# The seam between output projection and second MLP: first weights unpacked inside the join's loop, the last tiles turned at other places, other banks and another order of products

## The chip, the cores and the metric

The kernel runs on one core of a Trainium2 chip. The metric is the device time of one execution in microseconds (us). Engines are named as in the profile: PE is TensorE's matrix multiply and PEld its weight load, DVE is VectorE, ACT is ScalarE, POOL is GpSimd, and SP is SyncE, which issues nearly all DMAs here. L215 means line 215 of the kernel.

## The reference, cut to what matters

Two residual layers on x of shape 2 x 1024 x 512 (2048 tokens, 16 tiles of 128 tokens), all in float32:

```
xn = layernorm(x)
s  = delta_rule_attention(xn)            # 16 heads of 128, then o @ Wo
g  = silu(ternary_mlp(xn))               # inner width 1408
x  = x + s * g
xn = layernorm(x)
s  = rg_lru(xn)                          # block-diagonal gates, softplus(a_param), a scan over time
g  = silu(nvfp4_mlp(xn))                 # inner width 4096, 4-bit codes with a scale per block of 32
x  = x + s * g
```

The seam of this case is the line in the middle: the output projection `o @ Wo`, its product with g, the sum with x and the layernorm, and the beginning of the second layer's MLP.

## The kernel before

**First layer.** A long loop over units of the attention computes the heads' outputs and writes them to a DRAM buffer `od`; the first MLP runs woven into it and leaves its gated result in `gd`. This loop is planned by the kernel's own code and isn't touched by the diff.

**The join** (class `Join`). For each of the 16 tiles of tokens (two batches alternate, `self.order`), `product` (L186 on) multiplies the 16 heads' outputs by the resident `wo`, in 16 matmuls of 128x128 by 128x512 (two records each) that add up in one PSUM bank `jpo`. Then `rest` holds the steps after it: `jg = jg * jpo` (L215, DVE), `jx = jg + jx` (L211, DVE; a DMA writes it to `x1d`), statistics of the layernorm (L206 to L208, DVE), `ln_rs = ve ** -0.5` (L218, POOL), and the norm, written over `jg` (L219, DVE). `turn` transposes the normed tile twice on PE (`ptr`, L113, 4 + 4 matmuls): one copy (ACT, L117) goes to DRAM `xd` for the recurrence, one (DVE, L119) goes into the "quarters" `xq[b]` that the second MLP reads, and for every second tile of a batch four DVE adds (L261 to L264) make sums of these quarters. The first three tiles' products are made at the end of the attention's loop, woven into it; `Join.run` (L222) does the rest, a tile per iteration, with loads of `jo` (L173), `jx` (L182) and `jg` (L184) two or three tiles ahead. In an iteration `run` issues product i, the steps of `rest`, and then, as `late`, the turn of tile i-1, so on PE the transposes of tile i-1 stand behind the whole product i. The norm of the last tile is a tile of its own, `xn_last`, and its turn is returned and done by the second layer.

**Second layer** (`second_layer`, L1079). The MLP's 4096 inner columns are worked off in 16 groups. A group's weights w_g, w_u and w_d come as 4-bit codes `pk` with scales `sc`; `unpack` (L1119) loads both and then yields after each of seven DVE operations (five on the codes' bits, with `hi` as a second buffer, and two multiplications by `sc`), after which POOL makes four sums of blocks of the weights (3.65 us in all). The products are of a Strassen kind: seven products of quarters, so that weights and `xq` each exist in seven pieces. A half step n of the main loop (L1441 on; 32 of them, group n // 2, batch n % 2) is the gate's seven products and the up projection's seven, 14 slots in all. In each slot the code takes one product, one piece of the down projection of the half step before (`downs`), one step of the next group's unpacking (`steps`), and pieces of the recurrence, which has 16 chunks that start at half steps set by `starts` (`recur`). From `order["on"] = True` on, engines do their instructions in the order in which the program writes them (class `Ordered`, whose helper line L130 is the line of all of these in the profile); ahead of that a scheduler of the compiler's framework places them. In the last group the sums of the down projection's seven parts, `together`, are put between, one per slot.

Ahead of the main loop stand, in this order: the first group's unpacking (three weights, 24 steps), loads of `bd` and `vec`, and `softplus` (L87 on) of `vec`: two ACT functions and some 18 small DVE operations on 128x4. PSUM pools are `l1_psh` (banks of the gate and up products: pga, pgb, pgc, pua, pub, puc), `l1_pso` and `l1_psr`, allocated in this order; they take the place of the join's banks.

The names that the change touches are `Join.run`, `Join.turn`, `second_layer` with `unpack`, `quartered`, `halved` and `group_weights`, and its main loop.

Of the kernel before, what the change touches and what calls it, by code (L numbers as in the profile page):

```python
# [4 lines left out]

# [7 lines left out]
F32 = mybir.dt.float32  # L13
# [4 lines left out]
ALU = mybir.AluOpType  # L18
PSUM = bass.MemoryType.PSUM
DRAM = bass.MemoryType.DRAM  # L20

P = 128
B, T, D = 2, 1024, 512
NT = B * T
KC = D // P
NTT = NT // P
H = 16
# [35 lines left out]
def done(steps):  # L63
    for _ in steps:
        pass
# [72 lines left out]
class Join:  # L138
# [86 lines left out]
    def run(self, xd, xq, xp):  # L225

        nc, tc = self.tc.nc, self.tc
        with self.ctx as ctx:
            ps_o, ps_t = (
                ctx.enter_context(tc.tile_pool(name=n, bufs=bufs, space=PSUM, reuse_waits="tile"))  # L230
                for n, bufs in (("j_pso", 3), ("j_pst", 2))
            )
            late = None
            for i in range(NTT):
                if i >= self.made:
                    for _ in range(min(i + 3, NTT) - len(self.o)):
                        self.load_o()
                    done(self.product(ps_o, "pso", nc.tensor.matmul))
                    g = self.xg[i][1]
                    if i == NTT - 1:  # L240
                        g = xp.tile([P, D], F32, name="xn_last")
                    for step in self.rest(g):
                        step()
                if late is not None:
                    late(ps_t, "pst", self.xg[i - 1][0].rearrange("p (k t) -> p k t", k=KC))
                    for _ in range(min(i + 3, NTT) - len(self.xg)):
                        self.load_xg()
                g = g if i == NTT - 1 else self.xg[i][1]
                late = functools.partial(self.turn, xd, xq, *self.order[i], g)
        return late  # L250

    def turn(self, xd, xq, c, b, g, psp, tag, xt):
        nc, ident = self.tc.nc, self.cst[:, C_ID, :]
        transposed(nc, psp, tag, xt, g, ident, "scalar")
        nc.sync.dma_start(xd[b].rearrange("k p t -> p k t")[:, :, c * P : (c + 1) * P], xt)
        h, cols = c % 2, slice(c // 2 * P, (c // 2 + 1) * P)
        quarters = xq[b][:, 0:4].rearrange("p (kc h) par t -> p h kc par t", h=2)[:, h, :, :, cols]
        transposed(nc, psp, tag, quarters, g, ident, "vector", step=2)
        if h:
            b11, b12, b21, b22, t1, t2, t4 = (xq[b][:, q, :, cols] for q in range(7))  # L260
            nc.vector.tensor_tensor(t1, b12, b11, ALU.subtract)  # L261
            nc.vector.tensor_tensor(t2, b22, t1, ALU.subtract)
            nc.vector.tensor_tensor(t4, b21, t2, ALU.subtract)
            nc.vector.tensor_tensor(b12, b22, b12, ALU.subtract)  # L264
# [814 lines left out]
def second_layer(ctx, tc, a, cst, x1d, xd, xq, out, late):  # L1079
# [18 lines left out]
    nc = tc.nc  # L1098
    cp = ctx.enter_context(tc.tile_pool(name="l1_c", bufs=1, reuse_waits="tile"))
    rp = ctx.enter_context(tc.tile_pool(name="l1_r", bufs=1, reuse_waits="tile"))  # L1100
    wp = ctx.enter_context(tc.tile_pool(name="l1_w", bufs=2, side="right", reuse_waits="tile"))
    qp = ctx.enter_context(tc.tile_pool(name="l1_q", bufs=2, side="right", reuse_waits="tile"))
    hp = ctx.enter_context(tc.tile_pool(name="l1_h", bufs=1, reuse_waits="tile"))
    ps_h = ctx.enter_context(tc.tile_pool(name="l1_psh", bufs=1, space=PSUM, reuse_waits="tile"))
    ps_o = ctx.enter_context(tc.tile_pool(name="l1_pso", bufs=2, space=PSUM, reuse_waits="tile"))
    ps_r = ctx.enter_context(tc.tile_pool(name="l1_psr", bufs=2, space=PSUM, reuse_waits="tile"))
    yd = tc.dram_tile([NT, D], F32, name="yd")
    ident = cst[:, C_ID, :]
    order = {"on": False}
    PE, DVE, ACT, POOL = (  # L1110
        Ordered(tc, e, lambda: order["on"]) for e in (nc.tensor, nc.vector, nc.scalar, nc.gpsimd)
    )
    A11, A12, S3, A22, S1, S2, S4 = range(7)
    B11, T3, B21, B22, T1, T2, T4 = range(7)

    def unpack(name, g, dst, sums):  # L1119

        pk = qp.tile([P, 512], I32, tag="pk", name=f"pk_{name}_{g}")
        nc.sync.dma_start(pk, a[name + "pk"][g])
        sc = qp.tile([P, 512], F32, tag="sc", name=f"sc_{name}_{g}")
        nc.sync.dma_start(sc, a[name + "sc"][g])
        yield
        hi = qp.tile([P, 512], I32, tag="hi", name=f"hi_{name}_{g}", bufs=1)
        DVE.tensor_scalar(hi, pk, 0xF0, 12, ALU.bitwise_and, ALU.logical_shift_left)
        yield
        DVE.scalar_tensor_tensor(
            pk, in0=pk, scalar=0xF, in1=hi, op0=ALU.bitwise_and, op1=ALU.bitwise_or  # L1130
        )
        yield
        DVE.tensor_scalar(hi, pk, 0x00070007, 9, ALU.bitwise_and, ALU.logical_shift_left)
        yield
        DVE.tensor_scalar(pk, pk, 0x00080008, 12, ALU.bitwise_and, ALU.logical_shift_left)
        yield
        DVE.tensor_tensor(pk, pk, hi, ALU.bitwise_or)
        yield
        halves = pk.bitcast(F16).rearrange("p (n par) -> p par n", par=2)
        for par in range(2):  # L1140
            to = dst(par)
            k = to.shape[1]
            DVE.scalar_tensor_tensor(
                to,
                in0=halves[:, par, :].rearrange("p (k n) -> p k n", k=k),
                scalar=16384.0,
                in1=sc.rearrange("p (k n) -> p k n", k=k),
                op0=ALU.mult,
                op1=ALU.mult,
            )  # L1150
            yield
        for s in sums:
            POOL.tensor_tensor(*s)

    def quartered(name, g):

        w = wp.tile([P, 7, 2, P], F32, tag=f"w_{name}", name=f"w_{name}_{g}")
        a11, a12, a21, a22, s1, s2, s4 = (w[:, q] for q in range(7))
        sums = (
            (s1, a21, a22, ALU.add),  # L1160
            (s2, s1, a11, ALU.subtract),
            (a21, a11, a21, ALU.subtract),
            (s4, a12, s2, ALU.subtract),
        )
        return w, unpack(name, g, lambda par: w[:, 0:4, par, :], sums)

    def halved(g):


        w = wp.tile([P, 7, 256], F32, tag="w_d", name=f"w_d_{g}")  # L1170
        b11, b12, b21, b22, t1, t2, t4 = (w[:, q] for q in range(7))
        sums = (
            (t1, b12, b11, ALU.subtract),
            (t2, b22, t1, ALU.subtract),
            (b12, b22, b12, ALU.subtract),
            (t4, b21, t2, ALU.subtract),
        )
        return w, unpack("d", g, lambda par: w[:, 2 * par : 2 * par + 2], sums if g < NG - 1 else ())

    def group_weights(g):  # L1180
        (wg, s0), (wu, s1), (wd, s2) = quartered("g", g), quartered("u", g), halved(g)
        return (wg, wu, wd), itertools.chain(s0, s1, s2)

    weights, steps = group_weights(0)
    done(steps)


    bd = cp.tile([P, 2, KC, P], F32, name="bd")
    nc.sync.dma_start(bd, a["bd"])
    vec = cp.tile([P, 3, KC], F32, name="vec")  # L1190
    nc.sync.dma_start(vec, a["vec"])

    spa = cp.tile([P, KC], F32, name="spa")
    softplus(nc, cp, spa, vec[:, 0, :], 1.0, ("e", "w", "w2"))
    m4 = cp.tile([P, KC], F32, name="m4")
    nc.vector.tensor_scalar(m4, spa, 4.0, None, ALU.mult)
    carry = cp.tile([P, 1], F32, name="carry")

    def recur(kc, b, half):

# [232 lines left out]
    halves = [(kc, b, half) for b in range(B) for kc in range(KC) for half in range(2)]  # L1433
    starts = {1 + i * 27 // 15: h for i, h in enumerate(halves)}
    none = iter(())
    order["on"] = True
    before, recurring, downs, tog = None, none, none, none
    steps = none
    for n in range(2 * NG):
        g, b = n // 2, n % 2  # L1440
        if b == 0:  # L1441
            wg, wu, wd = weights
            done(steps)
            if g < NG - 1:
                weights, steps = group_weights(g + 1)
        if n == 2 * NG - 2:
            for _ in range(4):
                load_last()
        if g == NG - 1:
            tog = together(b)  # L1450
        lasts = none
        if n == 2 * NG - 1:
            lasts = down_last(0, wd)
        for f, products in enumerate(up_and_gate(g, b, wg, wu)):
            for s in range(7):
                slot = 7 * f + s
                if s == 1:
                    if before:
                        before()
                else:  # L1460
                    products[s - (s > 0)]()
                if n == 0 and slot == 3:
                    late(ps_r, "psr", rp.tile([P, KC, P], F32, tag="y", name="xt_last"))
                next(downs, None)
                if slot < 10:
                    next(lasts, None)
                next(steps, None)
                if g == NG - 1:
                    next(tog, None)
                if slot == 7 and n in starts:  # L1470
                    recurring = recur(*starts[n])
# [109 lines left out]
```

## Time and profile before

| | us |
|---|---|
| three runs | 3243.4, 3247.23, 3242.52 (median 3243.4) |
| the profiled execution, its own time | 3248.6 |
| its span | 3246.8 |
| PE busy | 3169.7 (98% of the span) |
| DVE busy | 2142.2 (66%) |
| ACT busy | 1245.7 (38%) |
| POOL busy | 824.1 (25%) |

The attention's loop ends in the neighbourhood of 1830 us, the join's loop at 2022, and the second MLP runs from there to 3237. A profile line of the timeline gives start, duration, engine, line, operation, output and inputs by the names of the program, sizes, and in brackets how long the engine was idle before and what released it. The list of waits gives what an engine waited for: total us, number of times, and the longest. The span is divided by the page in 40 slices, with PE's granted clock in tenths for each.

### The profile page before, as it was taken

Reading aid. Unit: us, or ns where it says so; the run is one execution under the profiler, and the core shown is the slowest. Engines: PE = TensorE matmul, PEld = TensorE weight load, DVE = VectorE, ACT = ScalarE, POOL = GpSimd, SP = SyncE. Lnnn points to the kernel's source line nnn. Section 1 sums busy time; section 2 is a strip of 40 time slices with the busy share of each in tenths; the row PEclk is TensorE's granted clock in tenths of the full one; section 3 lists DMA queues with packets and bytes.
Section 4 is the critical chain, followed back from the end, with each engine's and each line's share of the span. In section 5 each row is a group of like instructions: output and inputs, shape, how many; then the busy total and the mean of one; then the engine's idle time right before and its main releaser. Section 6 shows DMA issues by size and latency. Waiting matters only on the chain. (4 is left out here: it accounts for less than half of the span.)

```text
span 3246.8 us, 38192 instructions
## 1 busy us (share of the span) xinstructions
PE 3169.7 (98%) x12454; PEld 1958.8 (60%) x12454; DVE 2142.2 (66%) x4286; ACT 1245.7 (38%) x2259; POOL 824.1 (25%) x1204
## 2 busy tenths in 40 slices
PE   7999999999999999998999999999999999999998
PEld 6566756666666666665666544555555555555554
DVE  4566578786877777675555324676677666766676
ACT  3475445556555555444443100222222222322223
POOL 2000022322222223222322101323323323323222
PEclk9999999999999999999999999999999999999999
DMA  6244334444444443434323444111001100100014
GB/s 180 63 140 107 96 109 112 113 129 128 118 110 133 132 127 105 104 106 131 85 72 100 135 136 132 36 33 33 26 26 33 33 26 26 39 26 26 26 36 130
DMA packets 498246, 281.11 MB, mean 87 GB/s; under 512 B 206848, under 2 KB 443136, under 8 KB 498048
## 3 DMA queue, kind: packets, MB, share of 16 engines
q1 hardware_dynamic: 490048, 265.83, 29.2%
q0 software_dynamic: 5696, 8.65, 0.9%
q10 hardware_dynamic: 2304, 4.20, 0.4%
q8 instruction: 99, 1.62, 0.2%
q14 instruction: 99, 0.81, 0.1%
HBM read 179.71 MB, written 86.25 MB: 82 GB/s over the span
## 5 line engine op out<-in xcount | busy, mean ns | idle before, releaser
L130 DVE TENSOR_TENSOR acc<-acc,po 128x512 f32<-128x512 f32 x408 | 278.2, 682 | 219.9 <-PE po L130 218.8
L130 PEld LDWEIGHTS po<-w_d,i 128*128 128x128 f32 x1024 | 194.5, 190 | 143.6 <-issue 113.3
L130 PE MATMUL po<-w_d,i 128*128 128x256 f32 (+1 forms) x1024 | 275.4, 392 | 0.8 <-DVE i L130 0.8
L130 PE MATMUL pga<-xq,w_g 128*128 128x512 f32 x512 | 244.2, 600 | 8.6 <-ACT g L130 4.5
L130 PE MATMUL pgate<-xnT,wg 128*128 128x512 f32 x512 | 248.6, 595 | 0.0
L130 PE MATMUL pwv<-xnT,wv 128*128 128x512 f32 x512 | 245.0, 594 | 1.8 <-ACT gate L130 1.8
L130 PE MATMUL pwq<-xnT,wq 128*128 128x512 f32 x512 | 245.2, 594 | 0.0
L130 PE MATMUL pwk<-xnT,wk 128*128 128x512 f32 x512 | 240.2, 600 | 2.3 <-ACT ka L130 2.3
L130 PE MATMUL pua<-xq,w_u 128*128 128x512 f32 x512 | 240.7, 592 | 0.0
L130 ACT COPY g<-pga 128x512 f32<-128x512 f32 x96 | 56.2, 585 | 442.4 <-PE pga L130 435.2
L130 DVE SCALAR_TENSOR_TENSOR v<-prewv,cw,v 128x512 f32<-128x512 f32 x192 | 169.5, 884 | 65.1 <-ACT v L130 53.1
L130 PEld LDWEIGHTS po<-w_d,s 128*128 128x128 f32 x720 | 136.8, 190 | 95.4 <-issue 85.1
L130 PE MATMUL po<-w_d,s 128*128 128x256 f32 x720 | 184.8, 379 | 0.0
L130 ACT COPY w<-zw 128x128 f32<-128x128 f32 x192 | 50.6, 264 | 340.4 <-PE zw L130 340.1
L198 PE MATMUL jpo<-wo,jo 128*128 128x512 f32 x416 | 181.0, 592 | 0.0
L130 POOL TENSOR_TENSOR rs<-rs,minus_half 128x4 f32<-128x4 f32 x64 | 64.4, 1007 | 427.6 <-DVE rs L130 397.5
L130 PEld LDWEIGHTS zw<-rr,ground 128*128 128x128 f32 x512 | 97.1, 193 | 125.2 <-issue 98.5
L130 DVE SCALAR_TENSOR_TENSOR ka<-prewk,cw,ka 128x512 f32<-128x512 f32 x192 | 148.1, 773 | 36.1 <-ACT ka L130 26.8
L130 DVE TENSOR_TENSOR rr<-rr,zw 128x128 f32<-128x128 f32 x192 | 54.8, 285 | 176.3 <-PE zw L130 174.8
L130 DVE SCALAR_TENSOR_TENSOR q<-prewq,cw,q 128x512 f32<-128x512 f32 x192 | 160.0, 833 | 14.4 <-ACT q L130 7.9
L130 POOL TENSOR_TENSOR ot<-ot,gate 128x512 f32<-128x512 f32 x64 | 86.7, 1355 | 300.2 <-ACT ot L130 270.8
L130 ACT ACT_TABLE_LOAD x115 | 147.5, 1283 | 14.5 <-PE pr L130 11.3
(242 smaller groups left out, 6605.6 us busy)
## 6 DMA issues: line engine op xcount, KB each, us to landing
e<-gr SPq DMA_DIRECT2D x64, 256.0 KB, 4.1
de<-e SPq DMA_DIRECT2D x64, 256.0 KB, 2.7
dk<-ka SPq DMA_DIRECT2D x32, 512.0 KB, 2.8
kb<-dk SPq DMA_DIRECT2D x64, 256.0 KB, 3.4
eb<-de SPq DMA_DIRECT2D x64, 256.0 KB, 3.0
eg<-egr SPq DMA_DIRECT2D x64, 256.0 KB, 3.9
od<-ot SPq DMA_DIRECT2D x64, 256.0 KB, 2.1
jo<-od SPq DMA_DIRECT2D x16, 1024.0 KB, 6.2
```

The source lines that it names most:

```text
L130: i = getattr(self.engine, name)(*args, **kw)
L198: matmul(po, lhsT=ot[:, h, :], rhs=self.wo[h], start=(h == 0), stop=(h == H - 1))
```

## The change

- In `Join.run` the product is issued in two halves of eight heads each (`itertools.islice(product, H // 2)`), and the turn of tile i-1 stands between them. Tiles whose product was made earlier are turned as before. `turn` takes the engines as an argument.
- In `second_layer` the buffers of weights have a pool each (`l1_wg`, `l1_wu`, `l1_wd`), `vec` and softplus's buffers one of their own (`l1_v`), and `l1_psh` is allocated as the last of the PSUM pools instead of the first, so its tiles lie in other banks.
- `bd`, `vec` and softplus are written ahead of the first group's unpacking instead of after it; softplus writes into `m4` (`spa` is gone).
- Loading a weight's codes (`packed`) is parted from unpacking. A group's steps are now: load g and u (one step), seven for w_g, load d and seven for w_u, seven for w_d: 22 instead of 24. The framework's scheduler places the first group's steps: w_g and w_u, with `vec` and softplus, come to stand at the start of the join's loop, between tiles 2 and 3; the two last operations of w_d come at the post-processing of the last tile but one.
- In the first half step the gate's first six products are taken in the order 1, 3, 2, 5, 4, then the last tile's turn, then 6; it was 1 to 6, with the turn written after the third and left to the scheduler. This turn is now in program order on its engines.
- In the main loop the next group's unpacking skips slots 0, 2 and 4 of half steps in which a chunk of the recurrence is at work (`active`), and `together` takes two pieces in each of slots 0 to 2 of the last group's half steps.

The diff, cut to its core:

```diff
@@ Join.run
-                    done(self.product(ps_o, "pso", nc.tensor.matmul))
+                    product = self.product(ps_o, "pso", nc.tensor.matmul)
+                    done(itertools.islice(product, H // 2))
+                    if late is not None:
+                        late(nc, ps_t, "pst", self.xg[i - 1][0].rearrange("p (k t) -> p k t", k=KC))
+                    done(product)
                     g = self.xg[i][1]
...
+                elif late is not None:
+                    late(nc, ps_t, "pst", self.xg[i - 1][0].rearrange("p (k t) -> p k t", k=KC))
                 if late is not None:
-                    late(ps_t, "pst", self.xg[i - 1][0].rearrange("p (k t) -> p k t", k=KC))
@@ second_layer
-    wp = ctx.enter_context(tc.tile_pool(name="l1_w", bufs=2, side="right", reuse_waits="tile"))
-    qp = ctx.enter_context(tc.tile_pool(name="l1_q", bufs=2, side="right", reuse_waits="tile"))
+    vp = ctx.enter_context(tc.tile_pool(name="l1_v", bufs=1, side="right", reuse_waits="tile"))
+    qp, *wps = (
+        ctx.enter_context(tc.tile_pool(name=n, bufs=2, side="right", reuse_waits="tile"))
+        for n in ("l1_q", "l1_wg", "l1_wu", "l1_wd")
+    )
...
-    ps_h = ctx.enter_context(tc.tile_pool(name="l1_psh", bufs=1, space=PSUM, reuse_waits="tile"))
     ps_o = ctx.enter_context(tc.tile_pool(name="l1_pso", bufs=2, space=PSUM, reuse_waits="tile"))
     ps_r = ctx.enter_context(tc.tile_pool(name="l1_psr", bufs=2, space=PSUM, reuse_waits="tile"))
+    ps_h = ctx.enter_context(tc.tile_pool(name="l1_psh", bufs=1, space=PSUM, reuse_waits="tile"))
...
+    ordered = types.SimpleNamespace(tensor=PE, vector=DVE, scalar=ACT, sync=nc.sync)
...
-    def group_weights(g):
-        (wg, s0), (wu, s1), (wd, s2) = quartered("g", g), quartered("u", g), halved(g)
-        return (wg, wu, wd), itertools.chain(s0, s1, s2)
-
-    weights, steps = group_weights(0)
-    done(steps)
+    def group_weights(g, w):
+
+        g_, u_ = packed("g", g), packed("u", g)
+        yield
+        wg, steps = quartered("g", g, *g_)
+        yield from steps
+        d_ = packed("d", g)
+        wu, steps = quartered("u", g, *u_)
+        yield from steps
+        wd, steps = halved(g, *d_)
+        yield from steps
+        w += wg, wu, wd
...
-    vec = cp.tile([P, 3, KC], F32, name="vec")
+    vec = vp.tile([P, 3, KC], F32, name="vec")
     nc.sync.dma_start(vec, a["vec"])
-    spa = cp.tile([P, KC], F32, name="spa")
-    softplus(nc, cp, spa, vec[:, 0, :], 1.0, ("e", "w", "w2"))
-    m4 = cp.tile([P, KC], F32, name="m4")
-    nc.vector.tensor_scalar(m4, spa, 4.0, None, ALU.mult)
+    m4 = vp.tile([P, KC], F32, name="m4")
+    softplus(nc, vp, m4, vec[:, 0, :], 1.0, ("e", "w", "w2"))
+    nc.vector.tensor_scalar(m4, m4, 4.0, None, ALU.mult)
     carry = cp.tile([P, 1], F32, name="carry")
+    weights = []
+    done(group_weights(0, weights))
@@ main loop of second_layer
+    def last_turn():
+        late(ordered, ps_r, "psr", rp.tile([P, KC, P], F32, tag="y", name="xt_last"))
+
...
         if b == 0:
+            done(steps)
             wg, wu, wd = weights
-            done(steps)
...
+        active = n - 1 in starts
...
-                if s == 1:
-                    if before:
-                        before()
+                if n == f == 0:
+
+                    (products[:1] + products[2:3] + products[1:2] + products[4:5] + products[3:4]
+                     + (last_turn, products[5]))[s]()
+                elif s == 1:
+                    before()
                 else:
                     products[s - (s > 0)]()
-                if n == 0 and slot == 3:
-                    late(ps_r, "psr", rp.tile([P, KC, P], F32, tag="y", name="xt_last"))
                 next(downs, None)
                 if slot < 10:
                     next(lasts, None)
-                next(steps, None)
-                if g == NG - 1:
+                if slot not in (0, 2, 4) or not active:
+                    next(steps, None)
+                for _ in range(1 + (slot < 3) if g == NG - 1 else 0):
                     next(tog, None)
```

More of the change, by code (lines that the diff above doesn't have):

```diff
@@ L3 @@
 import math
+import types
 from contextlib import ExitStack
@@ L250, in run, with turn @@
         return late
-    def turn(self, xd, xq, c, b, g, psp, tag, xt):
-        nc, ident = self.tc.nc, self.cst[:, C_ID, :]
+    def turn(self, xd, xq, c, b, g, nc, psp, tag, xt):
+        ident = self.cst[:, C_ID, :]
         transposed(nc, psp, tag, xt, g, ident, "scalar")
@@ L1100, in second_layer @@
     rp = ctx.enter_context(tc.tile_pool(name="l1_r", bufs=1, reuse_waits="tile"))
-    wp = ctx.enter_context(tc.tile_pool(name="l1_w", bufs=2, side="right", reuse_waits="tile"))
-    qp = ctx.enter_context(tc.tile_pool(name="l1_q", bufs=2, side="right", reuse_waits="tile"))
+    vp = ctx.enter_context(tc.tile_pool(name="l1_v", bufs=1, side="right", reuse_waits="tile"))
[3 more added lines that the diff above has]
+    )
+    wps = dict(zip("gud", wps))
     hp = ctx.enter_context(tc.tile_pool(name="l1_h", bufs=1, reuse_waits="tile"))
-    ps_h = ctx.enter_context(tc.tile_pool(name="l1_psh", bufs=1, space=PSUM, reuse_waits="tile"))
     ps_o = ctx.enter_context(tc.tile_pool(name="l1_pso", bufs=2, space=PSUM, reuse_waits="tile"))
     ps_r = ctx.enter_context(tc.tile_pool(name="l1_psr", bufs=2, space=PSUM, reuse_waits="tile"))
+    ps_h = ctx.enter_context(tc.tile_pool(name="l1_psh", bufs=1, space=PSUM, reuse_waits="tile"))
     yd = tc.dram_tile([NT, D], F32, name="yd")
@@ L1112, in second_layer, with packed @@
     )
+    ordered = types.SimpleNamespace(tensor=PE, vector=DVE, scalar=ACT, sync=nc.sync)
     A11, A12, S3, A22, S1, S2, S4 = range(7)
     B11, T3, B21, B22, T1, T2, T4 = range(7)
-    def unpack(name, g, dst, sums):
+    def packed(name, g):
         pk = qp.tile([P, 512], I32, tag="pk", name=f"pk_{name}_{g}")
@@ L1124, in unpack @@
         nc.sync.dma_start(sc, a[name + "sc"][g])
-        yield
+        return pk, sc
+    def unpack(name, g, pk, sc, dst, sums):
         hi = qp.tile([P, 512], I32, tag="hi", name=f"hi_{name}_{g}", bufs=1)
@@ L1153, in unpack, with quartered @@
             POOL.tensor_tensor(*s)
-    def quartered(name, g):
-        w = wp.tile([P, 7, 2, P], F32, tag=f"w_{name}", name=f"w_{name}_{g}")
+    def quartered(name, g, pk, sc):
+        w = wps[name].tile([P, 7, 2, P], F32, tag=f"w_{name}", name=f"w_{name}_{g}")
         a11, a12, a21, a22, s1, s2, s4 = (w[:, q] for q in range(7))
@@ L1164, in quartered, with halved @@
         )
-        return w, unpack(name, g, lambda par: w[:, 0:4, par, :], sums)
-    def halved(g):
-        w = wp.tile([P, 7, 256], F32, tag="w_d", name=f"w_d_{g}")
+        return w, unpack(name, g, pk, sc, lambda par: w[:, 0:4, par, :], sums)
+    def halved(g, pk, sc):
+        w = wps["d"].tile([P, 7, 256], F32, tag="w_d", name=f"w_d_{g}")
         b11, b12, b21, b22, t1, t2, t4 = (w[:, q] for q in range(7))
@@ L1177, in halved @@
         )
-        return w, unpack("d", g, lambda par: w[:, 2 * par : 2 * par + 2], sums if g < NG - 1 else ())
-    def group_weights(g):
-        (wg, s0), (wu, s1), (wd, s2) = quartered("g", g), quartered("u", g), halved(g)
-        return (wg, wu, wd), itertools.chain(s0, s1, s2)
-    weights, steps = group_weights(0)
-    done(steps)
+        sums = sums if g < NG - 1 else ()
+        return w, unpack("d", g, pk, sc, lambda par: w[:, 2 * par : 2 * par + 2], sums)
+    def group_weights(g, w):
[9 more added lines that the diff above has]
+        w += wg, wu, wd
     bd = cp.tile([P, 2, KC, P], F32, name="bd")
     nc.sync.dma_start(bd, a["bd"])
-    vec = cp.tile([P, 3, KC], F32, name="vec")
+    vec = vp.tile([P, 3, KC], F32, name="vec")
     nc.sync.dma_start(vec, a["vec"])
-    spa = cp.tile([P, KC], F32, name="spa")
-    softplus(nc, cp, spa, vec[:, 0, :], 1.0, ("e", "w", "w2"))
-    m4 = cp.tile([P, KC], F32, name="m4")
-    nc.vector.tensor_scalar(m4, spa, 4.0, None, ALU.mult)
+    m4 = vp.tile([P, KC], F32, name="m4")
+    softplus(nc, vp, m4, vec[:, 0, :], 1.0, ("e", "w", "w2"))
+    nc.vector.tensor_scalar(m4, m4, 4.0, None, ALU.mult)
     carry = cp.tile([P, 1], F32, name="carry")
+    weights = []
+    done(group_weights(0, weights))
     def recur(kc, b, half):
@@ L1441, in second_layer @@
         if b == 0:
+            done(steps)
             wg, wu, wd = weights
-            done(steps)
             if g < NG - 1:
-                weights, steps = group_weights(g + 1)
+                weights = []
+                steps = group_weights(g + 1, weights)
         if n == 2 * NG - 2:
```

## The prediction

> **What bounds the kernel now.** I began with the page's busy shares and the waits of TensorE. Columns of the first line: busy us, share, instructions.
>
> ```profile
> PE 3169.7 (98%) x12454; PEld 1958.8 (60%) x12454; DVE 2142.2 (66%) x4286; ACT 1245.7 (38%) x2259; POOL 824.1 (25%) x1204
> ```
>
> PE is busy 98% of the span, and the diff leaves its products as they are in number and size. A gain can only be idle or half-speed time of PE. So I asked for PE's waits from the start of the join to the end, in two windows (1826 to 2100, 2050 to 3247; us in total, times, longest):
>
> ```profile
> PE pga L130 <- ACT g L130: 4.5, 1, 4.5
> PE pga L130 <- DVE jg L215: 4.1, 1, 4.1
> PE ptr L113 <- DVE xn_last L219: 1.0, 1, 1.0
> ```
>
> ```profile
> PE pgc L130 <- DVE g L130: 3.0, 10, 0.3
> PE po L130 <- DVE i L130: 0.8, 1, 0.8
> ```
>
> The first three are the seam, once each; the second window is the whole second MLP. The seam's timeline on PE (start, us, engine, line, operation, in brackets the idle time before and its releaser), then two lines each of DVE and ACT that release it:
>
> ```profile
> 2021.19 1.08 PE L113 MATMUL ptr<-cst,jg 128*128 128x128 f32 x8
> 2026.39 3.68 PE L130 MATMUL pga<-xq,w_g 128*128 128x512 f32 x4 [4.13 <-DVE jg L215]
> 2031.12 1.13 PE L113 MATMUL ptr<-cst,xn_last 128*128 128x128 f32 x8 [1.04 <-DVE xn_last L219]
> 2036.74 3.62 PE L130 MATMUL pga<-xq,w_g 128*128 128x512 f32 x4 [4.49 <-ACT g L130]
> 2040.20 1.88 PE L130 MATMUL pgc<-xq,w_g 128*128 128x512 f32 x4
> ```
>
> ```profile
> 2024.45 1.29 DVE L130 SCALAR_TENSOR_TENSOR w_d<-pk_d,sc_d 128x512 f32<-128x512 f16 x2
> 2025.66 0.68 DVE L215 TENSOR_TENSOR jg<-jpo,jg 128x512 f32<-128x512 f32 x1
> ```
>
> ```profile
> 2034.40 0.20 ACT L90 ACTIVATE sp_e<-vec 128x4 f32<-128x4 f32 x1 [2.01 <-DMA vec<-in_vec]
> 2034.63 1.28 ACT L91 ACT_TABLE_LOAD   x1
> ```
>
> The last join product is finished by 2021.2, but its multiply (L215), which frees its PSUM bank, runs at 2025.66, behind the unpacking of all three first weights on DVE. The first layer-two product stands on that bank. The next one stands behind an ACT copy, and ACT behind `vec`'s landing and a table load. Two products take 3.68 and 3.62 us where the same four matmuls follow at a pitch of 1.72. From 2022.27 (transposes done) to 2040.37 (full speed) are 18.1 us; two products at 1.72 and eight transposes at 1.08 are 4.5 us of work. **The seam loses 13.6 us**: 9.7 idle, 3.9 at half speed.
>
> [...] 3.68 and 3.62 for 1.72 after gaps of 4.13 and 4.49; none is slow in the steady part, where the gaps are 0.3. [...] `pk<-pk,hi` takes 0.69 us alone and 1.10 beside POOL's sums of weights.
>
> **The change part by part.**
>
> *Seam, removed.* The unpacking of w_g and w_u goes to the start of the join's loop, softplus and `vec` with it; only w_d's two last operations stay near the end (beside tile 14 of 0..15). The turn of tile i-1 stands between the halves of product i, so tile 14 is turned before the last product ends. The first product of layer two needs then a bank that an ACT copy freed, weights that are long there, and quarters of tile 12. I placed the rest from E, the end of the last product. Products in order first, third, second, fifth, fourth end at E+1.7, 3.4, 5.2, 6.9, 8.6. The chain of the last tile (multiply 0.68, add 0.69, statistics 0.68+0.17+0.15, POOL 0.55 to 0.66, norm 0.55) took 4.4 us at tile 13 (1992.08 to 1996.44), so `xn_last` is there at E+4.4, before its transposes at E+8.6. The sixth product follows at E+9.7 and needs a bank that a DVE add of `g` frees: ACT copies the fourth product at E+8.8 to 9.4, the add takes 0.69: about E+10.2, a wait of 0.5. Tile 14's own turn: w_d's two operations (1.29) and POOL's four sums (3.66) stand ahead of its `ln_rs` (0.66), so its norm comes about 7.7 after its product; PE is there after half a product, 6.9: a wait of 0.9. What is left of 13.6 is 1.4 to 1.5: **−12.1 us**. Bounds: −13.6 (no wait left) and −10 (the sixth product waits 1.5 and another 2 appear).
>
> *Slots of the second MLP.* The ten waits of 0.30 (2151.16, 2226.14 and on) recur where a chunk of the recurrence is active; a piece of unpacking stands on DVE ahead of the add of `g` for which PE waits. After, unpacking skips slots 0, 2 and 4 of active chunks, and it needs 22 steps instead of 24. There are 28 slots in a group, 25 with one active chunk, 22 with two, so it still ends in time. The piece (0.65 each of w_u's last two, more beside POOL) is out of the way of the add: all ten go, **−3.0 us**. Bounds 0 and −3.1; if only part clears, it's between.
>
> *Tail.* The single wait of 0.82 at the last w_d products: three adds of `acc` (0.68 each) are mixed with the adds of `i`. Two per slot in slots 0 to 2 bring them forward by three: **−0.8 us** (−0.2 to −1.2).
>
> *Start of the join's loop, added.* In before, PE doesn't wait here at all. Now DVE has between tile 2 and tile 3: w_g 0.43+0.69+0.43+0.42+0.69+1.29 = 3.95, the start of w_u, and softplus' 18 small operations (0.15 to 0.2) spread between. SyncE is moved past too: `vec`, pk_g, sc_g, pk_u are put between jx and jg loads, each waiting for earlier landings (xd 4.6 us, pk 2.7); I put pk_g's issue at 1840.95, its landing at 1843.65. From there w_g ends at about 1849.1 with eight small operations between, two operations of w_u at 0.4 to 1.1 follow, and tile 3's multiply runs at 1851.1, 4.7 us after its product (1846.4). Then its add, statistics and the rest of w_u alternate (0.68+0.83+1.0+0.42+0.68+0.69+0.17+0.65+0.15 and four small ones, less 0.1 of overlap at each): 1856.0; POOL and norm: about 1857. PE needs it after half of the next product, at 1846.4+6.9 = 1853.3. **+3.7 us** (2 to 6: with `vec` early it's 3.0, late 4.1). A gap of this length is that after which the trace shows half speed; [...] 1.7 us of loss at 0.75 is **+1.3 us**. The same chain at other tiles takes 4.4 to 4.6 us against a cover of 6.9; the cover's remainder is 2.3. Queued behind the late norm are jg and jx loads two tiles on, with over 10 us to their use: nothing.
>
> *At nothing.* The attention's own order is the same on all engines; loads of later weights, `bd` and `xc` are issued later and needed more than 10 us after; eight transposes cost 1.08 wherever they stand.
>
> Sum: −12.1 −3.0 −0.8 +3.7 +1.3 = **−10.9 us**. Against the profiled execution (span 3246.8, own time 3248.6) that is 3235.9 and 3237.7. The runs shown have a median of 3243.4, so I forecast 3243.4 − 10.9 = 3232.5.
>
> **Rivals.**
> *Loop start eats more.* [...] PE waits 6 to 9 us, tile 4 waits again as pk_d follows, and half clock comes in full. For it: POOL's sums of w_g (3.65) fall right on tile 3's chain. Against: the operations that share are five or six, at 0.4 more each, which is in my sum. Time: +9 to +13 instead of +5, so −3 to −7: 3236.5 to 3240.5.
> *Seam alone.* The slots' waits are not due to unpacking but to ACT's copy ahead of the add; they stay, the tail too: −12.1+5.0 = −7.1: 3236.3. For it: the waits are 0.30 each time, as of a fixed chain. Against: they come only in half of the chunks.
> *It doesn't do what it says.* First product or sixth still held, by a bank or `vec` in its new place: a new gap of 5 to 8 us with half clock eats what was gained: about 3243. Against: I found no such wait in the order of instructions.
> *Slower.* Turning inside product i leaves each tile's chain 6.9 us where it had a whole product of 14.7. It decides when chain to norm exceeds 6.9; it takes 4.5 now. At 8.0 for the twelve tiles of the loop it is 12 × 1.1 = +13, and with the start's +5 more than the seam gives: about 3246; at 8.5 about 3252. For it: loads of jg and jx are issued by the same queue that now has more in it. Against: the chain's pieces are bare durations with no queue in them.
>
> **How the numbers follow.** The sum as worked out 0.62 (its own range −14.5 to −7: 3229 to 3236.5), loop start 0.20, seam alone 0.06, nothing gained 0.06, slower 0.06. About 0.2%, or 6.5 us, is what a measurement of this kernel tells from no change: faster is below 3236.9. Faster 0.62+0.06 and half of 0.20: 0.78. Same: the other half and nothing gained: 0.16. Slower 0.06. The range takes the first three: 3228.5 to 3241; 0.06+0.06 and about 0.05 at the low end are left out.
>
> **What would show it.** Right: no gap over 1 us on PE between the last join product and the second MLP and all four-matmul records there at about 1.9; ten `pgc` waits gone; one gap of 3 to 4 us at the third or fourth tile's transposes, released by `jg` of L219's line, with PEclk below 1 there. Wrong: transposes waiting at several tiles; `pgc` or `po` waiting for DVE in every group; `pga` waiting first for a bank at the seam.

## The result, and the profile after

The changed kernel takes 3233.9 us (median of 6 runs, 3230.2 to 3237.9) where before takes 3244.9 (6 runs, 3242.5 to 3248.1): a ratio of 0.9965, 95% interval 0.9953 to 0.9978, or 11.1 us less. The forecast was 10.9 us less, and lies within the interval of −15 to −7 us.

The profiled executions differ by more, 3246.8 and 3228.4 us of span. So I cut both at four instructions that stand in the same place in each: the first group of eight transposes in the join (`ptr<-cst,jg ... x8`), the first product of the second MLP (`pga`), its first down product (`po`), and the last 32 records of `po`. Each entry is the difference of two starts in PE's timeline:

| us | before | after | difference |
|---|---|---|---|
| start to the first transposes x8 | 1829.72 | 1823.98 | −5.74 |
| join, to the first `pga` | 196.67 | 199.69 | +3.02 |
| seam, to the first `po` | 34.44 | 25.77 | −8.67 |
| second MLP, to the last `po` x32 | 1162.56 | 1155.86 | −6.70 |
| to the end | 23.41 | 23.10 | −0.31 |

The first row isn't the change's: the instructions there keep their order, and in the eleven kernels run below, all with the same attention, this mark lies anywhere from 1822.1 to 1829.3. (The lowest but one, 1822.79, is a kernel that differs from before in the second MLP alone.) What is left is −12.4 in the three middle rows, and these are sharp: 1155.86 comes back to the hundredth in ten of the eleven. The interval of the runs holds it. The join's row has two things in it: a new wait at the loop's start, and the 4.1 us for which the first `pga` waited before and now doesn't.

PE's waits from 1815 to 2060 in the changed kernel (us in total, times, longest); from 2045 to 3240 there are none, where before had eleven:

```profile
PE ptr L114 <- DVE jg L220: 4.4, 2, 4.1
PE pgc L131 <- DVE g L131: 0.6, 1, 0.6
```

The seam in PE's timeline (start, us, engine, line, operation, idle before):

```profile
2015.86 1.10 PE L114 MATMUL ptr<-cst,jg 128*128 128x128 f32 x8 [0.29 <-DVE jg L220]
2016.80 7.03 PE L199 MATMUL jpo<-wo,jo 128*128 128x512 f32 x16
2023.67 1.88 PE L131 MATMUL pga<-xq,w_g 128*128 128x512 f32 x4
2025.38 1.88 PE L131 MATMUL pgc<-xq,w_g 128*128 128x512 f32 x4
...
2032.25 1.07 PE L131 MATMUL ptr<-cst,xn_last 128*128 128x128 f32 x8
2033.90 1.96 PE L131 MATMUL pgc<-xq,w_g 128*128 128x512 f32 x4 [0.58 <-DVE g L131]
```

No product here takes 3.6 us any more; the 18.1 us have closed but for two short waits. The price stands at the loop's start:

```profile
1833.68 13.90 PE L199 MATMUL jpo<-wo,jo 128*128 128x512 f32 x32
1851.72 1.94 PE L114 MATMUL ptr<-cst,jg 128*128 128x128 f32 x8 [4.14 <-DVE jg L220]
1853.45 15.60 PE L199 MATMUL jpo<-wo,jo 128*128 128x512 f32 x32
1868.89 1.07 PE L114 MATMUL ptr<-cst,jg 128*128 128x128 f32 x8
```

The 32 records of one line here are the second half of one product and the first half of the next. The transposes of tile 3 wait 4.14 us, then take 1.94 for 1.08, and the product behind them 15.60 for 13.90: half speed. The granted clock in the trace is 0.50 from 1851.7 to 1855.0. DVE in that stretch, from tile 3's multiply to its norm:

```profile
1844.26 0.68 DVE L216 TENSOR_TENSOR jg<-jpo,jg 128x512 f32<-128x512 f32 x1
1844.86 0.15 DVE L99 SCALAR_TENSOR_TENSOR sp_e<-sp_e,sp_w 128x4 f32<-128x4 f32 x1
1844.93 0.96 DVE L131 TENSOR_SCALAR hi_u<-pk_u 128x512 int32<-128x512 int32 x1
1845.82 1.21 DVE L212 TENSOR_TENSOR jx<-jg,jx 128x512 f32<-128x512 f32 x1
...
1848.02 0.68 DVE L131 TENSOR_TENSOR pk_u<-pk_u,hi_u 128x512 int32<-128x512 int32 x1
...
1849.49 0.68 DVE L131 SCALAR_TENSOR_TENSOR w_u<-pk_u,sc_u 128x512 f32<-128x512 f16 x1
1850.63 0.94 DVE L220 TENSOR_SCALAR jg<-jx,ln_mv,ln_rs 128x512 f32<-128x512 f32 x1 [0.45 <-POOL ln_rs L219]
```

Every step of the tile's chain has a step of w_u and one of softplus between, so the norm ends 11.0 us after its product (which ended at 1840.55, half of the 32 records after 1833.68). PE has only 6.9 us of product to do in that time.

### The profile page after: what moved, and what is told of

The parts are those of the page before. It is cut to its first block, busy times and chain, and to the rows that moved or that the text cites. A ratio compares the mean times of both kernels' runs of the same rounds, so it can differ in the third digit from the quotient of the medians.

```text
span 3228.4 us, 38168 instructions
## 1 busy us (share of the span) xinstructions
PE 3162.7 (98%) x12454; PEld 1958.0 (61%) x12454; DVE 2145.3 (66%) x4286; ACT 1245.8 (39%) x2259; POOL 829.7 (26%) x1204
## 4 chain that ended last, share of the span: by engine, by line
PE 85%; DVE 5%; DMA 3%; issue 3%; ACT 2%; SPq 1%; POOL 1%; DVEq 0%; ACTq 0%; POOLq 0%
PE po L131 15%; PE pua L131 7%; PE pga L131 7%; PE pgate L131 6%; PE pwk L131 6%; PE pwq L131 5%; PE jpo L199 5%; PE pwv L131 4%; PE zw L131 4%; PE pgc L131 3%; PE puc L131 3%; PE pg L403 2%; PE pu L403 2%; PE po L426 2%; PE pub L131 2%
```

## The experiments

My theory after the result: the seam's gain comes of moving the unpacking, the steady waits go by the skipped slots, and the loop start's loss comes of unpacking and softplus on DVE ahead of a turn that has only half a product of cover. The rivals were that SyncE's queue or the turn's place sets the wait, that banks or order made the seam, and that the ten waits went by the shorter list of steps. Times are medians, beside those of before that were measured with them; "join" and "seam" are the rows of the table above.

**Operations held back.** A small DVE operation on one column reads a turned tile and writes the buffer that the first operation writes, so that this can't run earlier. w_g waits in this way for tile 4, w_u for 6, w_d for 8, and softplus, by the same function on its buffer `e` (not shown here), for tile 3:

```diff
+    def gate(dst, i):
+        c, b = i // 2, i % 2
+        x = xq[b][:, c % 2, 0, c // 2 * P : c // 2 * P + 1]
+        nc.vector.tensor_scalar(
+            dst.bitcast(I32), x.bitcast(I32), 0, 0, ALU.bitwise_and, ALU.logical_shift_left
+        )
...
         hi = qp.tile([P, 512], I32, tag="hi", name=f"hi_{name}_{g}", bufs=1)
+        if g == 0 and name in gates:
+            gate(hi[:, 0:1], gates[name])
```

> The changed kernel with softplus, w_g, w_u and w_d's first operations held back, each by one small DVE operation on 128x1 that reads tile 3, 4, 6 and 8 after its turn. My theory: the wait of 4.1 us at tile 3's transposes and the half speed after it come from these operations standing on DVE ahead of the tile's chain; held back, they fall into DVE's idle time between a turn and the next product's end. Then no wait of tiles 3 to 13 on PE, 6.6 us less than the changed kernel: about 3227 us, 0.9946 of before. Rival, the wait comes of the loads on SyncE's queue or of the turn's new place alone: a wait of 3 us or more stays at tile 3, about 3233. Rival, the work only moves: a wait of 2 to 4 us appears at tile 5, 7 or 9, about 3231.

Measured: 3223.9 us beside 3242.9, ratio 0.9943 (0.9930 to 0.9955). The join falls from 199.69 to 192.87 us, 6.82 less, seam and second MLP are the same to the hundredth (25.77, 1155.86). PE's waits between 1820 and 2060:

```profile
PE pgc L133 <- DVE g L133: 0.6, 1, 0.6
PE ptr L116 <- DVE jg L222: 0.3, 1, 0.3
```

The wait of 4.1 us is gone and appears at no other tile. So the cause is these operations' place on DVE; and each set of 4 us fits into DVE's idle time of one tile when it starts after the turn.

**Two turns put back.** The same operations at the same place, but with more cover:

```diff
                     done(itertools.islice(product, H // 2))
-                    if late is not None:
+                    if late is not None and (i > 4):
                         late(nc, ps_t, "pst", ...)
                     done(product)
...
-                elif late is not None:
+                if late is not None and (i < 3 or not (i > 4)):
                     late(nc, ps_t, "pst", ...)
```

> The changed kernel, but the turns of tiles 2 and 3 stand after the whole of the next product, as in before; tiles 4 to 14 are turned between the halves. Unpacking and softplus stay at the loop's start. My theory: tile 3's norm comes as late as in the changed kernel, but it has 14 us of cover instead of 6.9: no wait, no half speed, about 3227 us. Rival, the late chain pushes the next tile's: a wait of 1 us or more at tile 4's or 5's transposes, 3229 to 3232.

Measured: 3226.6 us, ratio 0.9950 (0.9934 to 0.9965); join 192.87, as in the kernel above. No tile waits but tile 14 (0.3). The late norm does no harm if a whole product hides it, and doesn't push later tiles. The loss needed both: the operations there, and the turn in mid-product.

**Softplus alone held back** (only its gate of the first diff).

> The changed kernel with softplus alone held back until tile 3 is turned; the three weights' unpacking stays. My theory, a sum of operations on DVE: 18 small operations fewer ahead of tile 3's norm at about 0.1 us each make the wait 2.2 to 2.8 us instead of 4.1, [...]: about 3230 us. Rival, the load of vec sets the beginning of the train: the wait falls to under 1 us, 3227. Rival, weights alone set it: 4 us stay, 3233.

Measured: 3228.9 us, ratio 0.9955 (0.9941 to 0.9969).

```profile
1853.46 1.94 PE L116 MATMUL ptr<-cst,jg 128*128 128x128 f32 x8 [2.89 <-DVE jg L222]
1855.19 16.00 PE L201 MATMUL jpo<-wo,jo 128*128 128x512 f32 x32
```

The wait is 2.89 instead of 4.14, just above the 2.2 to 2.8 that I expected: softplus has 1.25 us of it, the weights the rest. The half speed, which my 3230 us didn't contain, came here too (transposes 1.94 for 1.08, the product behind them 16.00 for 13.90), so the join takes 198.84, only 0.85 less than in the changed kernel.

**The slots of the second MLP as before.**

```diff
-                if slot not in (0, 2, 4) or not active:
-                    next(steps, None)
-                for _ in range(1 + (slot < 3) if g == NG - 1 else 0):
+                next(steps, None)
+                for _ in range(1 if g == NG - 1 else 0):
                     next(tog, None)
```

> The changed kernel with the second MLP's main loop taking one unpacking step in every slot and one piece of together per slot, as before; the first half step's order stays. My theory: the ten waits of the product pgc for DVE return, 0.30 us idle and 0.57 us of PE's pitch each, and the tail's wait of 0.8, 1.0 in pitch: 6.7 us more than the changed kernel, about 3240.5 us. Rival, the shorter list of steps (22 for 24) has moved the steps by one or two slots and is what cleared the waits: none or shorter ones come back, and only the tail costs 1.0: 3235.

Measured: 3246.1 us beside 3242.9, ratio 1.0010 (1.0004 to 1.0017): slower than before. The second MLP takes 1171.07 us, 15.2 more than in the changed kernel. Its waits from 2040 on:

```profile
PE pgc L131 <- DVE g L131: 7.4, 10, 0.7
PE po L131 <- DVE i L131: 0.8, 1, 0.8
PE po L131 <- DVE acc L131: 0.4, 1, 0.4
```

One of the ten in PE's timeline:

```profile
2139.02 1.88 PE L131 MATMUL pgb<-xq,w_g 128*128 128x512 f32 x4
2141.01 1.13 PE L131 MATMUL po<-w_d,i 128*128 128x256 f32 x4
2142.89 1.99 PE L131 MATMUL pgc<-xq,w_g 128*128 128x512 f32 x4 [0.74 <-DVE g L131]
2144.71 1.03 PE L131 MATMUL po<-w_d,i 128*128 128x256 f32 x4
```

In the changed kernel, where none of them waits (2136.73 to 2141.03), these four start 1.72, 0.86 and 1.72 us after each other; here it's 1.99, 1.88 and 1.82: 1.39 us lost where the list says 0.74. Ten of these and 1.0 at the tail are 14.9 of the 15.2. Both of my expectations missed: the shorter list, left alone, didn't clear the waits but made them longer. DVE ahead of the add of `g` in this kernel, at 2142.16:

```profile
2134.63 1.33 DVE L131 TENSOR_SCALAR hi_d<-pk_d 128x512 int32<-128x512 int32 x1
...
2137.21 0.68 DVE L131 SCALAR_TENSOR_TENSOR pk_d<-pk_d,hi_d 128x512 int32<-128x512 int32 x1
...
2140.88 0.63 DVE L131 TENSOR_SCALAR hi_d<-pk_d 128x512 int32<-128x512 int32 x1
```

Three pieces of w_d's unpacking, 2.64 us, stand in the slots ahead; in before it was one of w_u (1.59 at 2143.73) and one of w_d (0.68), 2.27 us, ahead of the same add, at 2150.44. This is one of the ten; the others aren't shown. Before's wait at that add, for comparison:

```profile
2149.84 1.03 PE L130 MATMUL po<-w_d,i 128*128 128x256 f32 x4
2151.16 1.98 PE L130 MATMUL pgc<-xq,w_g 128*128 128x512 f32 x4 [0.30 <-DVE g L130]
2152.99 1.03 PE L130 MATMUL po<-w_d,i 128*128 128x256 f32 x4
```

**The slots alone, put into before** (the opposite of the last diff, with before's 24 steps).

> The kernel before with the second MLP's slots alone changed: unpacking skips slots 0, 2 and 4 of active half steps, together takes two pieces in slots 0 to 2 of the last group; 24 steps, seam and join as before. Theory: the skipped slots alone clear the ten waits (0.57 us of pitch each) and the tail's (1.0): the stretch from the first down product to the last falls from 1162.6 to 1155.9 us, 6.7 us less, about 0.998 of before. Rival, only the skip together with 22 steps clears them: two steps are left over in groups with two active half steps and are done in one go at the group's start, a wait of 1 to 3 us there, twice; 1157 to 1162 us. Rival, the waits are due to the chain of ACT and DVE: ten stay, 1162.6.

Measured: 3234.6 us beside 3243.6, ratio 0.9974 (0.9963 to 0.9984). The second MLP takes 1155.86 us, exactly as in the changed kernel; the seam's waits of before are all there (34.23 us). So the skipped slots and the pairs of `together` are worth 6.70 us alone, and the number of steps is worth nothing to them.

**Banks, order and turns, one at a time.** First `l1_psh` again ahead of the other PSUM pools:

> The changed kernel with the PSUM pools in the old order, so that the first gate product's bank is one that the join's last product uses. Theory: the first product waits for the last tile's multiply (L216), which now runs 0.2 us after the last product and takes 0.69: a wait of 0.8 to 1.1 us at the seam, no half speed, 1.0 us more than the changed kernel. Rival, the bank was what held before's seam: 4 us and half speed come back, 6 to 8 us more.

Measured: 3227.5 us, ratio 0.9950 (0.9936 to 0.9964). The timeline at the seam and at tile 3:

```profile
2020.04 1.98 PE L131 MATMUL pga<-xq,w_g 128*128 128x512 f32 x4 [0.78 <-DVE jg L216]
```

```profile
1849.63 1.10 PE L114 MATMUL ptr<-cst,jg 128*128 128x128 f32 x8 [3.94 <-DVE jg L220]
```

The first product waits 0.78 us for the last multiply, as expected. That this kernel has a shorter time than the changed one isn't the banks' doing: tile 3 waits 3.94 us as there, but the transposes then take 1.10, not 1.94, and the product behind them 13.90, not 15.60. The join takes 197.94 us in spite of the 0.9 that the bank adds to it; without that it is 2.7 less than in the changed kernel. The shorter wait is 0.2 of this; the half speed, which the one execution has and the other not, is 2.5 (transposes 0.8, product 1.7 by the starts).

Then the first products in the old order:

```diff
-                if n == f == 0:
-
-                    (products[:1] + products[2:3] + products[1:2] + products[4:5] + products[3:4]
-                     + (last_turn, products[5]))[s]()
-                elif s == 1:
-                    before()
+                if s == 1:
+                    if before:
+                        before()
                 else:
                     products[s - (s > 0)]()
+                if n == 0 and slot == 3:
+                    last_turn()
```

> The changed kernel with the first half step's gate products in the old order 1, 2, 3, turn of the last tile, 4, 5, 6. Theory: the second product stands on the copy of the first one's bank (0.58 on ACT after the first's end): a wait of about 0.8; the last turn comes at E+6 where its norm is there at E+4.4: no wait; the fourth's and the sixth's waits are 0 to 0.6. 0.5 to 1.5 us more than the changed kernel in the seam. Rival: the order is what makes the seam; 4 us or more, with half speed.

Measured: 3229.6 us, ratio 0.9957 (0.9943 to 0.9970); seam 26.25 us, 0.48 more than with the new order: a wait of 0.72 at the second product, none at the last turn, and none that the list shows at the sixth product (where the new order has 0.58). Tile 3 waits 4.10 us.

Then all turns after the whole product (the second diff with no tile turned in mid-product):

> The changed kernel with all turns after the whole of the next product, as in before; unpacking stays at the loop's start. Theory: no wait at tile 3 (as with tiles 2 and 3 alone), and at the seam tile 14's quarters come 7.7 us later than in the changed kernel: its transposes end 1.1 us after the last product, and the second product to run needs their copy (0.7), the multiply of the last tile before it (0.7) and one or two adds: a wait of 1 to 2 us, no half speed; 5 us less than the changed kernel. Rival: the split is what makes the seam; a wait of 4 us with half speed there, no better than the changed kernel.

Measured: 3225.8 us, ratio 0.9945 (0.9932 to 0.9959). Join 192.78, seam 26.16: with the split turns and the operations held back it was 192.87 and 25.77, so the split is worth 0.3 us at the seam. I had expected 1 to 2.

**All three put back together**, so that of the seam's change only the place of unpacking and softplus is left (and their buffers).

> The changed kernel with turns after the whole product, PSUM pools and order of the first products all as in before; what stays of the seam's change is that unpacking and softplus run at the loop's start, in buffers of their own (and the second MLP's slots). Theory: moving these operations away is nearly the whole of the seam's gain; with the last multiply at once after its product, the old banks and order cost only a wait of about 1.3 at the second product (quarters of tile 14) and some tenths: the join and the seam together (first early transposes to first down product) take 220 to 221 us, against 231.1 of before and 218.6 with unpacking held back; about 3229 us. Rival: banks and order each held the seam, 4 us and half speed return: 225 to 229, 3235 or more.

Measured: 3225.6 us beside 3243.6, ratio 0.9941 (0.9928 to 0.9955). Join and seam together 218.91 us, where before has 231.11, the changed kernel 225.46, and the changed kernel with its operations held back 218.64. There is one wait from the join's start to the end:

```profile
2021.07 1.98 PE L131 MATMUL pga<-xq,w_g 128*128 128x512 f32 x4
2023.93 1.95 PE L131 MATMUL pga<-xq,w_g 128*128 128x512 f32 x4 [0.88 <-DVE ln_ve L209]
```

The move alone is worth 12.2 us, where all of the seam's changes with the operations held back had 12.5. Turns in mid-product, new banks and new order add 0.3 us to it at the seam, and the turns cost 6.8 at the loop's start. Not parted from the move were the buffers of their own and the earlier load of `vec`.

**The opposite: new turns, banks and order, but unpacking late** (the gates of the first diff at tile 13, softplus at 14).

> The changed kernel with the first unpacking held back to tile 13 and softplus to tile 14, about where before had them; split turns, new banks and new order stay. Theory: the tile 14's norm stands behind w_u's unpacking and POOL's sums and comes 10 us after its product, PE needs it after 6.9: a wait of 3 to 4 us with or without half speed, and later ones up to 1 us; join and seam together 222 to 225 us, 3230 to 3233 us in all. So place alone explains 4 to 6 us of the 12.5, and structure the rest when the place is bad. Rival: with split turns, banks and order the place doesn't matter: 219 to 220 us. Rival: the place is all: 229 to 231 us.

Measured: 3228.8 us, ratio 0.9952 (0.9936 to 0.9967). Join 198.48 and seam 25.77 are 224.25 us.

```profile
2012.39 1.94 PE L116 MATMUL ptr<-cst,jg 128*128 128x128 f32 x8 [3.04 <-DVE jg L222]
2014.12 9.11 PE L201 MATMUL jpo<-wo,jo 128*128 128x512 f32 x16
```

A wait of 3.0 at tile 14 and half speed (1.94 for 1.08, 9.11 for 7.03): the late place alone, with the structure left new, costs 5.6 us of the 12.5. What the structure is worth at before's own place isn't shown by this, for the place isn't before's. Unpacking begins here at 1996.56, 26.5 us before the last join product ends, in before at 2009.43, 11.8 us before it. So here the last multiply comes 8.6 us after w_d is done, where before has it at once behind w_d. Softplus and the load of `vec` are earlier than in before, too.

**The best version.** Everything held back as in the first experiment, and w_d's last operations, with their sums on POOL, held back until tile 14 is turned:

```diff
             k = to.shape[1]
+            if g == 0 and name == "d" and par == 0:
+                gate(to[:, 0, 0:1], 14)
             DVE.scalar_tensor_tensor(
```

> The changed kernel with unpacking and softplus held back to tiles 3, 4, 6 and 8, and the last operations of w_d and their sums on POOL held back until tile 14 is turned. Theory: the 0.3 us wait at tile 14's transposes goes, 0.5 us of PE's pitch; only the 0.6 us wait of pgc is left between the join's start and the last products: join 192.4 us, about 3223 us, 0.9941 of before. Rival: POOL's sums now meet the last tile's chain, a wait of 0.5 or more at its transposes.

Measured: 3223.5 us beside 3243.6, ratio 0.9938 (0.9926 to 0.9950): 20 us ahead of before. Join 192.38, seam 25.77: 7.3 us less than in the changed kernel, and 0.5 less than in the first experiment, which the runs alone don't tell apart (ratios 0.9938 and 0.9943). PE's waits from 1820 to the end:

```profile
PE pgc L133 <- DVE g L133: 0.6, 1, 0.6
```

## Why the prediction was right, point by point

The total was right to 0.2 us by the runs, and partly by luck: by the traces two terms were too small, with opposite signs, the loop's start by 1.8 us and the slots by 2.7. The waits that went and the one that came were those named.

- **Seam, −12.1.** It was −12.5: before's join and seam, 231.11, less 218.64 with the loop start's stall taken away. The steps held: `pga` starts at once after the last product; the wait of tile 14 was 0.29 (I had 0.9; its norm ended at 2015.7, 7.2 after its product and not 7.7, for POOL began the first sum between w_d's two operations), the sixth product's 0.58 (I had 0.5). My bounds held. What I gave as one term with the order, banks and turns, though, is nearly the move's alone: with all three undone 12.2 of the 12.5 stay.
- **Slots, −3.0.** All ten waits went, by the mechanism named (unpacking ahead of the add on DVE), shown by the slots alone in before. The size was wrong: −5.7. I took the idle time of the list, 0.30, as the price. In before's timeline, shown above, the product after the wait starts at 2151.16, where 2150.70 was due after `po` at 2149.84, and the one behind it comes 1.83 later instead of 1.72: 0.46 + 0.11 = 0.57 each. My upper bound of −3.1 was therefore too narrow. That 22 steps matter was wrong; only the skip does.
- **Tail, −0.8.** It was −1.0, by the same reading; the wait is gone. 5.7 and 1.0 are the whole of the row's 6.70.
- **Start of the loop, +3.7 and +1.3.** The wait was 4.14, or 4.3 by the starts around it, at tile 3 as named, released by `jg`'s norm. Two errors of mine partly cancelled in it. The multiply ran at 1844.26, 3.7 after its product, where I had 4.7. The load of pk_g wasn't early: it landed at 1838.5, 2.0 ahead of the product's end, where I had 2.75. But from the landing to the multiply DVE took 5.7 us and not 7.45. From the multiply to the norm's end, with the steps alternating, it took 7.3 where I had 5.9, so the norm ended 11.0 after the product, where I had 10.6. (Softplus has 16 small operations in the trace, not 18.) Half speed came in this execution and cost 2.5, where I had reckoned 1.7 for it: +6.8 for the term. The chance of 0.75 was my estimate, not a reading, and about right: of six kernels with a gap of 2.9 to 4.1 us (five at tile 3, one at tile 14), five show it.
- **At nothing.** Right: no wait of PE between tile 3 and tile 14, and none from later loads.

The sum by the traces is −12.5 + 6.8 − 5.7 − 1.0 = −12.4, by the runs −11.1; the difference is within their interval. Of the rivals, "loop start eats more" was right in its direction (+6.8 for +5.0) and short of its +9. "Seam alone" fell with the slots alone in before. "It doesn't do what it says" fell: the two waits left at the seam are 0.29 and 0.58. "Slower" fell: from multiply to norm the chain took 3.8 to 3.9 us at tiles 4 to 13, and there the cover of 6.9 was enough. The case that I had not weighed is that the change's own parts work against each other: the split turns, which bring 0.3 us, take the cover away that the moved unpacking needed.

## What to carry to other kernels

Work that is moved off a seam needs a place with cover, and the cover is measured from that engine's queue: here DVE has most of each tile's 14.65 us free (in the changed kernel three tiles in a row, from 1868.89 on, show it busy for 3.7 to 5.2), yet two weights and softplus in one go ahead of a tile's chain cost 6.8, and the same ones started after a turn, 4 us at a time, cost nothing. Price a wait by the starts of the instructions around it, not by its idle time: 0.30 in the list was 0.57 in the pitch, 0.74 was 1.39. And undo each part of a change alone: of four at this seam one carried the gain, and one took half of it back.

## What the runs showed of the hardware that was not expected

PE's half speed didn't go by the length of the gap alone. At the turns it followed gaps of 2.89 us (softplus alone held back), 3.04 (unpacking late), 3.59 (slots as before), 4.10 (old order) and 4.14 (changed kernel), each time with transposes at 1.94 for 1.08, but not one of 3.94 (old banks, 1.10).

The granted clock, read from the traces in steps of 0.2 us, is 0.50 in before from 2026.46 to 2029.87 and from 2033.28 to 2040.11. In the changed kernel it falls to 0.50 at 1850.04, 2.5 us after the end of PE's last product (1847.58). What sets these times, and why no half speed followed the gap of 3.94, these runs don't show.
